# Layer 1 of a two-layer graph network: six products on constants ahead of the transposes of each turn

## The chip, the cores and the metric

The kernel runs on one core of a Trainium2 chip. The metric is the device time of one execution in microseconds; the runs of a kernel are compared by their median. The engines are named as in the profile: PE (TensorE's products), PEld (TensorE's loads of the stationary operand), DVE (VectorE), ACT (ScalarE), POOL (GpSimd) and SP (SyncE, which here issues transfers).

## What is computed

There are 12500 nodes with 48 features and 400000 edges, sorted by their target. Two layers follow each other, each on the normalized, rectified features:

```python
h = jnp.maximum(_layernorm(x, axis=-1), 0.0)
x = x + _L0_gnn_ref(h, edge_index, L0_gnn_W, L0_gnn_b)
h = jnp.maximum(_layernorm(x, axis=-1), 0.0)
x = x + _L1_gnn_ref(h, edge_index, edge_attr_16, ...)
```

Layer 0 is a normalized sum over neighbours with one linear map. Layer 1, in which the change lies, is a small network on every edge and a mean over the edges of a target:

```python
edge = jnp.concatenate([x[source], x[target], edge_feat], axis=-1)
h = jax.nn.relu(edge @ W1 + b1)
h = jax.nn.relu(h @ W2 + b2)
message = h @ W3 + b3
msum = jax.ops.segment_sum(message, target, num_segments=n)
...
update = msum / jnp.maximum(cnt, 1.0)[:, None]
return x + update
```

## The kernel before

The first part of the kernel sorts the edges into runs and computes layer 0; it ends with tables in DRAM: `htab`, the rectified features h of each node, and `btab`, h times the target's part of W1. Then comes the loop of layer 1. It handles the edges in 782 turns c. A turn has four tiles of 128 edges (B = 4; the last turn has one). The steps of a turn are Python functions, and the loop calls them so that four turns are under way at once:

```python
for c in range(NC1 + 3):
    run.append(fetch(c) if c < NC1 else None)
    for step, late in ((summed, 3), (second, 2), (first, 1), (turn, 0)):
        if 0 <= c - late < NC1:
            step(run[c - late])
```

- `fetch(c)` brings in the data. Four indirect transfers that POOL issues (helper `gather`, L208) fetch the source's row of `htab` for each of 128 edges into `et`; these are called the gathers here. ACT copies the edge features into the same tile (L934). DVE compares the targets with the numbers of a window of 40 nodes and writes the result into rows 64 to 103 of the tile `mv` (helper `window_of`, L596), and makes the one-hot tile `oh` for the sum (L941). Once in eight turns SP loads the targets of eight turns, repeated over 40 partitions, into `db` (helper `targets`, L578, 640 KB), with a small load from `wtab_i`, and ACT issues the load of the edge features of eight turns (L923, 256 KB). Every second turn SP loads 40 rows of `btab` into a weight tile (L931).
- `turn` transposes the four tiles of `et` on PE into the PSUM tile `et_ps` (L953), and ACT copies it into rows 0 to 63 of `mv` (L954).
- `first` multiplies `mv` by the weights on PE, 512 edges at once (L959); ACT adds the bias and rectifies (L963).
- `second` multiplies by W2 on PE, four products of 128 columns (L970); DVE takes the maximum with the negative of the bias (L974 and L975).
- `summed` adds the edges into the window's 40 nodes on PE with `oh` as the stationary operand (L990). Every second turn ACT copies the sum out (L999) and SP stores it (L1000).

All of layer 1's operands on PE are f32; layer 0's two products per tile (L793 and L809) are bf16. The profile shows an f32 product as two loads and two passes, a transpose as one.

A scheduler sets the order of each engine's instructions and adds the waits; within an engine the order is fixed. On PE a turn reads: four transposes of turn c, then `summed`, `second` and `first` of the turns behind it, then the transposes of c + 1. On DVE it reads L974, L941, L975, L596. L596 writes a buffer of `mv` that L959 read, so it waits for a product of `first`. The pools have eight buffers of `et`, four of `mv`, and two each of `et_ps` and the other PSUM tiles, which fill all eight banks of PSUM. A gather waits until the transposes of the turn eight before it have read its buffer.

After the loop the two tables of sums are loaded again, multiplied by W3, divided by the counts and added to x.

Of the kernel before, what the change touches and what calls it, by code (L numbers as in the profile page):

```python
# [9 lines left out]
BF = mybir.dt.bfloat16  # L10
# [5 lines left out]
P = 128  # L16
# [4 lines left out]
def kernel(  # L21
# [32 lines left out]
    nc = tc.nc  # L54
# [12 lines left out]
    B = 4  # L67
# [170 lines left out]
    with tc.tile_pool(name="runs", bufs=1) as rp, tc.tile_pool(  # L238
        name="runs_ps", bufs=2, space=bass.MemoryType.PSUM
# [156 lines left out]
    with tc.tile_pool(name="begin", bufs=1) as bp_, tc.tile_pool(  # L396
        name="begin_ps", bufs=1, space=bass.MemoryType.PSUM
# [58 lines left out]
        with tc.tile_pool(name="ln0", bufs=2) as lp, tc.tile_pool(  # L456
            name="ln0_ps", bufs=2, space=bass.MemoryType.PSUM
# [187 lines left out]
    with tc.If(fast > 0) as branch:  # L645
# [6 lines left out]
        with tc.tile_pool(name="tiles", bufs=2) as wp, tc.tile_pool(  # L652
            name="tiles_ps", bufs=2, space=bass.MemoryType.PSUM
# [6 lines left out]
            for h0 in range(0, NS, HG):  # L660
# [31 lines left out]
                for h in range(n):  # L692
# [9 lines left out]
                    for g in range(NC8):  # L702
# [4 lines left out]
                            start=(g == 0),  # L707
                            stop=(g == NC8 - 1),
# [14 lines left out]
            for k in range(2):  # L723
# [5 lines left out]
                    start=True,  # L729
                    stop=True,  # L730
# [13 lines left out]
        with tc.tile_pool(name="e0", bufs=4) as wp, tc.tile_pool(  # L744
            name="n0", bufs=2
# [107 lines left out]
    with branch.Else():  # L853
        with tc.tile_pool(name="deg", bufs=2) as dp, tc.tile_pool(
            name="deg_ps", bufs=1, space=bass.MemoryType.PSUM
# [27 lines left out]
        with tc.tile_pool(name="s0", bufs=2) as wp, tc.tile_pool(  # L883
            name="s0_ps", bufs=1, space=bass.MemoryType.PSUM
# [21 lines left out]
    with tc.If(fast > 0) as branch:  # L906
        with tc.tile_pool(name="e1", bufs=3) as wp, tc.tile_pool(
            name="e1_ps", bufs=2, space=bass.MemoryType.PSUM
# [4 lines left out]
            for k in range(WB):  # L913
                nc.sync.dma_start(wk[k][:F], w1[:F])
                nc.sync.dma_start(wk[k][F:64], w1[2 * F :])
            ea_view = edge_attr[:E4].rearrange("(c p j) f -> p c j f", p=P, j=B)
            def fetch(c):
                n = B if c < NCH else TAIL
                if c % VG == 0:
                    group["db"] = targets(wp, 64, c)  # L920
                    v = min(VG, NCH - c)
                    ea = wp.tile([P, VG, B, EF], FP, name="ea", bufs=2)
                    nc.scalar.dma_start(ea[:, :v], ea_view[:, c : c + v])  # L923
                    group["ea"] = ea
                db, ea = group["db"], group["ea"]
                if c == NCH:
                    nc.scalar.dma_start(ea[:, c % VG, 0, :], edge_attr[E4:])
                if c % Q == 0:
                    group["at"] = window_at(db, 64, c)
                    wc = wk[c // Q % WB]  # L930
                    nc.sync.dma_start(wc[64:], btab[bass.ds(group["at"], W), :])  # L931
                at, wc = group["at"], wk[c // Q % WB]
                et = wp.tile([P, B, 64], FP, name="et", bufs=8)
                nc.scalar.activation(et[:, :n, F:], ea[:, c % VG, :n, :], AF.Copy)  # L934
                for j in range(n):
                    t = c * B + j
                    gather(et[:, j, :F], htab, src_i[:, t : t + 1])
                mv = wp.tile([K1, B * P], FP, name="mv", bufs=4)
                window_of(db, 64, c, mv[64:, : n * P])
                oh = wp.tile([P, B, W], FP, name="oh", bufs=6)  # L940
                nc.vector.tensor_tensor(  # L941
                    oh[:, :n],
                    rel[:, c * B : c * B + n].unsqueeze(2).to_broadcast([P, n, W]),
                    iota_f[:, None, :W].to_broadcast([P, n, W]),
                    OP.is_equal,
                )
                return dict(c=c, n=n, at=at, wc=wc, et=et, mv=mv, oh=oh)

            def turn(k):
                n, et, mv = k["n"], k["et"], k["mv"]  # L950
                et_ps = ps.tile([64, B * P], FP, name="et_ps")
                for j in range(n):
                    nc.tensor.transpose(et_ps[:, j * P : (j + 1) * P], et[:, j, :], ident)  # L953
                nc.scalar.activation(mv[:64, : n * P], et_ps[:, : n * P], AF.Copy)  # L954
# [48 lines left out]
# [5 lines that stand above are left out]
        with tc.tile_pool(name="m1", bufs=2) as npool, tc.tile_pool(  # L1008
            name="m1_ps", bufs=2, space=bass.MemoryType.PSUM
# [39 lines left out]
    with branch.Else():  # L1049
        with tc.tile_pool(name="s1", bufs=2) as wp, tc.tile_pool(  # L1050
            name="s1_ps", bufs=1, space=bass.MemoryType.PSUM
# [3 lines left out]
            with tc.For_i(0, NT, 1) as iv:  # L1055
# [9 lines left out]
                et_ps = ps.tile([IN1, P], FP, name="et_ps")  # L1065
# [72 lines left out]
```

## Time and profile before

| | |
|---|---|
| median of nine runs | 6188.61 us (6176.88 to 6193.04) |
| the profiled execution | 6170.85 us, with a span of 6169.0 us from the first to the last instruction |
| gathers of layer 1, first start to last end | 2054.2 to 6045.8 us, 3125 of them |
| mean of a gather | 972 ns |
| busy in the whole span: PE, PEld | 4410.7 us (71%), 3335.8 us (54%) |
| busy in the whole span: DVE, ACT, POOL | 3164.2 us (51%), 2301.0 us (37%), 3164.1 us (51%) |
| mean clock granted to TensorE | 0.944 of full speed |

A row of a group gives the line, the engine, the operation, the tile it writes and the tiles it reads, the number of instructions, then the busy time and the mean of one in ns, then the idle time of the engine just before them and what ended most of it. A row of the timeline gives the start in us, the duration in us, the engine, the line, the operation, and in brackets the idle time before it and what ended that. Several neighbouring instructions of one group stand in one row (x4).

### The profile page before, as it was taken

How to read it: one execution, taken by the hardware profiler on the slowest of the kernel's cores; microseconds unless marked ns; L12 is line 12 of the kernel's file. 1: busy time of each engine (PE TensorE's matmuls, PEld its weight loads, DVE VectorE, ACT ScalarE, POOL GpSimd, SP SyncE). 2: the span in 40 equal slices, each digit the busy share in tenths (PEclk: the TensorE clock that was granted, in tenths of full speed). 3: DMA queues.
4: the chain of work that ended last, by engine and by line, in shares of the span. 5: the costliest groups of instructions: out<-in, count | busy, mean ns of one | idle time of the engine just before them, and what ended most of it. 6: DMA issues, size and time to landing. Idle time of an engine off the chain costs nothing.

```text
span 6169.0 us, 97254 instructions
## 1 busy us (share of the span) xinstructions
PE 4410.7 (71%) x35368; PEld 3335.8 (54%) x35368; DVE 3164.2 (51%) x4843; ACT 2301.0 (37%) x4904; POOL 3164.1 (51%) x3239
## 2 busy tenths in 40 slices
PE   0001559999999777777777777777777777777776
PEld 0001449999999555555555555555555455554555
DVE  3898489999999433333333333333333333333333
ACT  0001228888888432333323332332333322333331
POOL 0000700000000577777777777777777777777771
PEclk9999869999999899999999999999999999999996
DMA  2002134444444222222222222222222222222224
GB/s 69 2 0 99 31 81 151 147 146 147 147 146 146 65 48 46 48 44 48 48 46 45 47 48 46 48 44 48 46 48 44 48 48 46 46 46 48 47 40 105
DMA packets 397107, 407.58 MB, mean 66 GB/s; under 512 B 227481, under 2 KB 350957, under 8 KB 392110
## 3 DMA queue, kind: packets, MB, share of 16 engines
q1 hardware_dynamic: 155238, 273.99, 15.6%
q0 software_dynamic: 103488, 85.03, 8.0%
q10 hardware_dynamic: 137894, 42.24, 2.9%
q8 instruction: 283, 4.64, 0.3%
q14 instruction: 204, 1.67, 0.1%
HBM read 362.97 MB, written 38.02 MB: 65 GB/s over the span
## 4 chain that ended last, share of the span: by engine, by line
DMA 30%; PE 22%; POOL 16%; DVE 14%; issue 9%; ACT 6%; another core or an unknown queue 2%; POOLq 0%; ACTq 0%; DVEq 0%
DMA et<-htab,src_i 29%; POOL et L208 15%; PE u_ps L990 7%; ACT rows L797 5%; PE sum L809 3%; PE et_ps L953 3%; DVE kb L346 3%; DVE ka L346 3%; PE h_ps L970 3%; DVE ohs L781 2%; PE at_ps L793 2%; DVE oht L777 1%; PE h_ps L959 1%; DVE ohr L695 1%
## 5 line engine op out<-in xcount | busy, mean ns | idle before, releaser
L208 POOL DMA_INDIRECT et<-htab,src_i x3125 | 3038.7, 972 | 2228.5 <-PE tb L636 1275.5
L953 PE MATMUL et_ps<-ident,et 128*64 128x128 f32 x3125 | 690.7, 288 | 942.4 <-DMA et<-htab,src_i 929.8
L953 PEld LDWEIGHTS et_ps<-ident,et 128*64 128x64 f32 x3125 | 347.8, 111 | 1667.0 <-DMA et<-htab,src_i 998.3
L963 ACT ACTIVATE h<-h_ps,b_sb 128x512 f32<-128x512 f32 x782 | 537.2, 687 | 1600.7 <-PE h_ps L959 1599.2
L809 PE MATMUL sum<-rows,ohs 128*128 128x144 bf16 x10976 | 1008.5, 228 | 20.4 <-ACT rows L797 17.4
L797 ACT ACTIVATE rows<-at_ps 128x432 bf16<-128x432 f32 x1830 | 953.9, 531 | 144.7 <-DVE g L756 35.1
L974 DVE MEMSET h<- 128x4 f32 x782 | 48.5, 62 | 1839.5 <-PE u_ps L990 1839.5
L970 PE MATMUL h_ps<-w_sb,h 128*128 128x128 f32 x6250 | 981.3, 304 | 0.5 <-ACT h L963 0.5
L970 PEld LDWEIGHTS h_ps<-w_sb,h 128*128 128x128 f32 x6250 | 827.5, 206 | 169.4 <-ACT et L934 132.1
L990 PE MATMUL u_ps<-h,oh 128*40 128x129 f32 x6250 | 912.9, 292 | 0.0
L809 PEld LDWEIGHTS <-ohs 128*128 128x128 bf16 x10976 | 855.4, 144 | 25.8 <-issue 19.4
L975 DVE TENSOR_TENSOR h<-h_ps,b_neg 128x512 f32<-128x512 f32 x782 | 540.6, 691 | 585.4 <-PE h_ps L970 585.4
L954 ACT ACTIVATE mv<-et_ps 64x512 f32<-64x512 f32 x782 | 459.7, 588 | 984.9 <-PE et_ps L953 984.7
L959 PE MATMUL h_ps<-mv,wk 104*128 104x512 f32 x1564 | 824.6, 609 | 0.0
L781 DVE TENSOR_TENSOR ohs<-lo_b,iota_x 128x4096 bf16<-128x4096 bf16 (+1 forms) x350 | 786.0, 2246 | 51.1 <-PE sum L809 32.8
L990 PEld LDWEIGHTS u_ps<-h,oh 128*40 128x40 f32 x6250 | 678.5, 122 | 123.4 <-issue 34.3
L793 PE MATMUL at_ps<-g,oht 112*128 112x144 bf16 x5488 | 651.3, 226 | 35.9 <-DVE oht L777 35.5
L596 DVE TENSOR_SCALAR mv<-db,wid 40x512 f32<-40x512 int32 x782 | 534.3, 684 | 181.2 <-PE h_ps L959 170.9
L793 PEld LDWEIGHTS <-oht 112*128 112x128 bf16 x5488 | 416.2, 98 | 39.0 <-issue 35.9
L468 PE MATMUL tp<-ident,ht 128*48 128x128 f32 x98 | 25.7, 415 | 415.1 <-ACT ht L383 415.1
L208 POOL DMA_INDIRECT fine<-ltab,where_i x50 | 46.7, 934 | 506.4 <-ACT h_t L470 491.4
L941 DVE TENSOR_TENSOR oh<-rel,iota_f 128x160 f32<-128x160 f32 x782 | 256.1, 328 | 13.3 <-DMA wk<-in_L_gnn_W_dram 2.7
(190 smaller groups left out, 2374.3 us busy)
## 6 DMA issues: line engine op xcount, KB each, us to landing
at<-dltab SPq DMA_DIRECT2D x343, 448.0 KB
db<-in_dst_dram SPq DMA_DIRECT2D x97, 640.0 KB
et<-htab,src_i POOLq DMA_INDIRECT x3125, 2.4
ea<-in_edge_attr_dram ACTq DMA_DIRECT2D x97, 256.0 KB
utab<-zero SPq DMA_DIRECT2D x14, 903.0 KB
utab<-u SPq DMA_DIRECT2D x391, 20.2 KB
wk<-btab SPq DMA_DIRECT2D x391, 20.0 KB
uk<-utab SPq DMA_DIRECT2D x7, 903.0 KB
```

What stands on the lines that cost most here:

```text
L208: nc.gpsimd.indirect_dma_start(out=into, out_offset=None, in_=table, in_offset=bass.IndirectOffsetOnAxis(ap=idx, axis=0),)
L596: nc.vector.tensor_scalar(to.rearrange("p (j i) -> p j i", j=n), db[p0 : p0 + W, a : a + n * P].rearrange("p (i j) -> p j i", j=n), wid[p0 ...
L781: nc.vector.tensor_tensor(ohs[:, :n], lo_b[:, h0 : h0 + n, None, c : c + CG].to_broadcast([P, n, S, CG]), iota_x[:, None].to_broadcast([P, ...
L793: nc.tensor.matmul(ps3[:, i, :], oht[:, k, c % CG, :], g3[:, c, :], start=True, stop=True)
L797: nc.scalar.activation(rows[:, : len(tiles)], ps3[:, : len(tiles)], AF.Copy)
L809: nc.tensor.matmul(sums[k][:, j, :], ohs[:, k, j * P : (j + 1) * P, c % CG], rows[:, i, :], start=(c == 0 and j == 0), stop=(c == ND - 1 a ...
L953: nc.tensor.transpose(et_ps[:, j * P : (j + 1) * P], et[:, j, :], ident)
L959: nc.tensor.matmul(h1_ps[:, : n * P], k["wc"], k["mv"][:, : n * P], start=True, stop=True)
L963: nc.scalar.activation(h1[:, : n * P], h1_ps[:, : n * P], AF.Relu, bias=b1_sb)
L970: nc.tensor.matmul(h2_ps[:, j, :], h1[:, j * P : (j + 1) * P], w2_sb, start=True, stop=True)
L975: nc.vector.tensor_tensor(h2[:, :n, :H], h2_ps[:, :n], b2_neg[:, None, :].to_broadcast([P, n, H]), OP.max,)
L990: nc.tensor.matmul(u_ps, oh[:, j, :], h2[:, j, :], start=(q == 0 and j == 0), stop=(q == Q - 1 and j == n - 1),)
```

## The change

Ahead of the loop, DVE sets a bf16 tile `fill` of 128 x 512 to zero. In each turn, ahead of the four transposes, PE multiplies this tile by its own first 64 columns six times, into the PSUM tile `et_ps` that the transposes of that turn then overwrite. Each product has 128 rows, 64 stationary columns and 512 moving columns; nothing reads their results. In the changed kernel the lines behind the insertions are numbered 3 higher in `fetch` and 5 higher below the loop over the products; L596, in a helper above, keeps its number.

```diff
@@ -913,6 +913,9 @@
             for k in range(WB):
                 nc.sync.dma_start(wk[k][:F], w1[:F])
                 nc.sync.dma_start(wk[k][F:64], w1[2 * F :])
+            fill = wp.tile([P, B * P], BF, name="fill", bufs=1)
+            nc.vector.memset(fill, 0.0)
+            FILL = 6
             ea_view = edge_attr[:E4].rearrange("(c p j) f -> p c j f", p=P, j=B)
@@ -949,6 +952,8 @@
             def turn(k):
                 n, et, mv = k["n"], k["et"], k["mv"]
                 et_ps = ps.tile([64, B * P], FP, name="et_ps")
+                for _ in range(FILL):
+                    nc.tensor.matmul(et_ps, fill[:, :64], fill, start=True, stop=True)
                 for j in range(n):
                     nc.tensor.transpose(et_ps[:, j * P : (j + 1) * P], et[:, j, :], ident)
                 nc.scalar.activation(mv[:64, : n * P], et_ps[:, : n * P], AF.Copy)
```

## The prediction

> **What bounds the kernel now.** I read first the page, for the share of the layer-1 loop; then the table by stretches, for its ends and its clock; then the waits of POOL, to see whether anything holds up the gathers; last the timeline of a few turns, one instruction at a time. The page:
>
> ```profile
> span 6169.0 us, 97254 instructions
> ...
> L208 POOL DMA_INDIRECT et<-htab,src_i x3125 | 3038.7, 972 | 2228.5 <-PE tb L636 1275.5
> L953 PE MATMUL et_ps<-ident,et 128*64 128x128 f32 x3125 | 690.7, 288 | 942.4 <-DMA et<-htab,src_i 929.8
> ...
> L596 DVE TENSOR_SCALAR mv<-db,wid 40x512 f32<-40x512 int32 x782 | 534.3, 684 | 181.2 <-PE h_ps L959 170.9
> ```
>
> The gathers run from 2054 to 6046 us. The stretch's row, with busy time of PE, PEld, DVE, ACT and POOL, then the granted clock:
>
> ```profile
> 2054.00:6046.00 3992.00, 3049.71 (x17140) 2033.36 (x17140) 1377.77 (x3125) 1202.62 (x2731) 3038.67 (x3125) 0.95 0.23 47
> ```
>
> What POOL waited for between 2100 and 6040 us (total, times, longest):
>
> ```profile
> POOL et L208 <- issue: 719.0, 2359, 0.3
> POOL et L208 <- PE u_ps L990: 88.7, 291, 0.3
> POOL et L208 <- DMA et<-htab,src_i: 66.1, 217, 0.3
> ```
>
> Whatever name stands there, the pause between two gathers is 0.30 us. So POOL is never held up: 3125 gathers of 0.972 us and 0.30 us between them are 3975 us, the stage but for its first turns. A turn (four gathers) takes 5.00 us at the shortest, 4 x (0.945 + 0.305), and 5.10 on average. PE waits for the landings (942 us on L953); its work isn't the bound.
>
> But the gathers are not all alike. Timeline of a late turn and the one after it, POOL and L596 alone:
>
> ```profile
> 3933.95 0.95 POOL L208 DMA_INDIRECT et<-htab,src_i  x1 [0.31 <-issue]
> ...
> 3935.05 0.69 DVE L596 TENSOR_SCALAR mv<-db,wid 40x512 f32<-40x512 int32 x1 [0.82 <-PE h_ps L959]
> ...
> 3935.20 1.36 POOL L208 DMA_INDIRECT et<-htab,src_i  x1 [0.30 <-PE et_ps L953]
> ...
> 3938.12 1.13 POOL L208 DMA_INDIRECT et<-htab,src_i  x1 [0.31 <-issue]
> ...
> 3938.45 0.68 DVE L596 TENSOR_SCALAR mv<-db,wid 40x512 f32<-40x512 int32 x1 [0.17 <-PE h_ps L959]
> ```
>
> A gather that should take 0.945 us takes 1.36 and 1.13 where L596 lies badly. Call p the time from the start of the latest gather to the start of L596. Over all 782 turns of the timeline: with p from 0.14 to 0.43 that gather is longer by p - 0.13 (**first place**: 0.33 gives 0.19); with p from 0.68 to 1.15 the next gather is longer by p - 0.68 (**second place**: 1.10 gives 0.42); elsewhere nothing. These sum to 82 us of the 84 by which the gathers exceed 3125 x 0.945. So what can change the time is where L596 falls, and L596 starts 0.2 us after the last pass of `first` (L959): PE sets it.
>
> The Trainium skill's GPSIMD Engine Reference, section Specifications, says that GpSimd's SBUF interfaces are shared with VectorE, with contention from instructions in a 2-port mode or with two SBUF inputs. It would count L941 too; in the trace a gather beside L941 alone is longer by 0.15 us at most, nearly always by nothing. I count L596 alone.
>
> **How PE places L596 today.** In an ordinary turn PE waits for the fourth gather's landing; L596 starts 3.30 us after the last transpose, always at nearly the same p: 464 turns have p between 0.56 and 0.87, and cost 0.033 us each (15 us). After a late landing PE runs without waiting, and L596 comes every 3.40 us (3935.05 to 3938.45). In 140 turns L596 comes over 5.6 us after the one before it, in sum 342 us later than at 5.0; most follow the 640 KB load of db, issued once in 8 turns, 0.71 us after L596. 170 of these 342 us are the pieces from transposes to L596 that took some 4.9 us instead of 3.3, at half the granted clock after PE's wait. The other 318 turns cost 68 us.
>
> **The change, part by part.** The memset is one DVE instruction before the loop, 0.3 us, beside the first gathers' latency. In the order of instructions, six load-and-multiply pairs stand between `first` and the transposes of each of 782 turns; otherwise PE, DVE, ACT and POOL keep their order in the loop, and SP issues the small load of wtab_i a little sooner. The first product of a turn waits for its et_ps buffer, as the transposes did; ACT (L954) read that two turns earlier. The transposes still wait for the landings, now behind the products; behind them are the same `summed`, `second` and `first`, and with these L596.
>
> *Price of a product.* No bf16 product of 512 columns is in the trace. Nearest row: L959, two passes of 512 columns in f32, starts 0.433 us apart, 0.866 a product. In f32, 129 columns cost 0.224 us (L990, two passes 0.112 apart); in bf16, 144 columns cost 0.0645 (L809). Per column that is 1.74 against 0.45 ns, a factor of 3.9. So a product is 0.866/4 = 0.217 us by the nearest row, 0.229 by L809 stretched to 512 columns; six are 1.30 to 1.37. I take 1.30, since L959 has the same width. Could the loads not overlap? In L809 they do (load 0.144 busy, pair 0.0645). If none did, at 0.098 each (L793's), six would be 1.89: the far end.
>
> *What hides it.* PE waits about 1.6 us in an ordinary turn, from the end of `first` to the last landing, less the transposes. 1.30 fits in; 0.3 us is left, and p stays at 0.69. No wait goes away from POOL.
>
> *What it costs after a late landing.* PE's own turn is 3.40 + 1.30 = 4.70. L596 in the second place delays the next gather by p - 0.68, so the next p is p + 4.70 - 5.00 - (p - 0.68) = 0.38: the first place, and that for every such p. From the first place the next p is p + 4.70 - 5.00 - (p - 0.13) = -0.17, i.e. 1.08 after the gather before: the second place. A pair that repeats as long as PE is behind, at 0.25 + 0.40 = 0.65 us per two turns, 0.325 a turn. (With 3.40 the same formula gives 0.33 after the second place: the fence shows 3938.45 - 3938.12.) PE catches up 0.30 by itself and 0.325 because the gathers are slowed, 0.625 a turn, where it now has 1.6 and more. So 52% of all lateness becomes lengthened gathers.
>
> *Sum.* Lateness: 172 us without the half-clock pieces, 342 with all. The wait that precedes a half-clock piece was about 2.8 us and becomes 1.5, less than waits of ordinary turns now, so I leave out five sixths of the 170: 200 us. Catch-up turns: 200/0.625 = 320, cost 104 us; the other 462 at 0.033, 15 us. Together 119 against 82: +37. At the end, six products stand before the last transposes: at most +1.3, I count 1. Sum +38 us on the profiled execution, which took 6170.85 (span 6169.0): 6209. The median of the nine runs is 17.8 us above it; I put the same 38 on 6188.6: **6227 us**. Ends of this case: with 172 us, 89 + 17 - 82 = +24, and +10 if a quarter of that is caught up at rival A's pace; with all 342, 178 + 8 - 82 = +104, +105 with the tail.
>
> The Trainium skill's page TensorE: Matmul & The Clock Gate, section HAM oscillation, says that idle gaps over about 3.4 us throttle the array and that PE should be kept busy. The row agrees in kind: clock 0.95 in this stage. By that rule the change gains whatever half-clock time costs on the path, up to 170 us here; by the row of POOL's waits, that time is not on the path, and it gains 0.
>
> **Rivals.** *A, the pair breaks: faster.* If a turn is over 4.77 (products over 1.37 together, the upper end above), the p after the second place passes 0.45, where L596 no longer delays (0.43 still does, 0.47 doesn't). L596 then drifts over all places, 0.083 us a turn on average at this pace: 172/0.383 = 449 turns, 37 us, and 333 at 0.033, 11: 48 against 82, -34, so 6155. Nearer to 5.00 a turn it stays longer in the free places, down to nothing lost: -80, 6109. For it: the edge is only 0.07 us away. Against: L959 says 1.30. Decides at 4.77.
>
> *B, nothing to be seen.* Lateness is recovered by waits I do not foresee and pairs are rare: +1 from the tail, bounds -11 to +12, 6190. For it: POOL is the bound and PE has the room. Against: the fence shows both places one after the other already.
>
> *C, PE becomes the bound.* At 1.89, a turn takes 5.29: 782 x (5.29 - 5.10) = +149, 6338. It begins over 5.10, i.e. 1.70 for six. Against: the loads overlap in L809.
>
> **How the numbers follow.** Main case 0.64, A 0.18, B 0.12, C 0.06. About 0.2%, 12 us, is what a measurement of this kernel can tell from no change. Slower: main and C, less 0.02 for the main case's low end: 0.68. Within: B, that 0.02 and 0.01 of A: 0.15. Faster: 0.17. The range reaches from 6165, the upper part of A, over B to 6293, the main case's +105; it leaves out the rest of A and C. The main case alone: 6199 to 6294.
>
> **What would show it.** Right: gathers' mean up from 972 to about 983 ns (945 + 119 us/3125), pauses still 0.30; products starting 0.217 us apart; L596 every 4.70 us after a late landing, with p alternating near 0.38 and 1.08; clock near 1.0 in the stage. Wrong: products over 0.228 us, p past 0.45, a gather mean under 972 (A); mean unchanged (B); POOL pausing for PE (C).

## The result, and the profile after

The changed kernel takes 6205.83 us (median of 9 runs, 6200.75 to 6207.13). The kernel before, timed beside it in 29 runs, takes 6183.39. The ratio is 1.0034, with an interval of 1.0026 to 1.0042: some 21 us slower. The forecast was 38 us. The time lies in the range and the direction came as forecast, but the forecast size was nearly twice what came, and the direction came by a path that neither the main case nor a rival had (below). The profiled execution took 6196.64 us (span 6194.9).

The page of the changed kernel (busy time, mean of one, idle time ahead and its releaser):

```profile
span 6194.9 us, 105865 instructions
...
L208 POOL DMA_INDIRECT et<-htab,src_i x3125 | 3064.8, 981 | 2206.3 <-PE tb L636 1253.9
L956 PE MATMUL et_ps<-fill 128*64 128x512 bf16 x4692 | 1164.5, 384 | 4.9 <-DVE fill L917 4.0
...
L596 DVE TENSOR_SCALAR mv<-db,wid 40x512 f32<-40x512 int32 x782 | 569.3, 728 | 164.7 <-PE h_ps L964 155.6
L958 PE MATMUL et_ps<-ident,et 128*64 128x128 f32 x3125 | 517.1, 282 | 119.1 <-DMA et<-htab,src_i 118.8
```

The gathers' mean went from 972 to 981 ns, 26 us over 3125 gathers; the stage from the first gather's start to the last one's end went from 3991.6 to 4017.3 us; what lies behind it stayed at 123.2 us. PE's wait for the landings, 942 us in front of the transposes, is down to 119: the products fill it. L596 itself takes 728 ns in place of 684.

The same stretch of the table by stages (busy time of PE, PEld, DVE, ACT, POOL; granted clock; DMA share; GB/s):

```profile
2054.00:6046.00 3992.00, 3867.96 (x21682) 2296.70 (x21682) 1409.82 (x3110) 1213.53 (x2718) 3045.23 (x3105) 0.99 0.23 47
```

The clock rose from 0.95 to 0.99: the half-clock pieces of the stage fell from 108 (392 us) to 12 (51 us). That bought nothing. The rule that the prediction weighed, the Trainium skill's TensorE: Matmul & The Clock Gate, section HAM oscillation, is borne out in kind, for less idle time went with a higher clock. Its figure is not: of the 108 pieces before, only 4 came within 7 us after a wait of PE of over 3.4 us (the longest wait in those 7 us is 2.3 us in the median, where the prediction has 2.8), and the changed kernel still has such pieces though no wait of PE between 2100 and 6040 us is over 2.34 us. The time went the way of the row of POOL's waits. In the changed kernel's waits of POOL, 2100 to 6040 us, the pause is still 0.3 us, whoever is named:

```profile
POOL et L208 <- issue: 727.8, 2388, 0.3
POOL et L208 <- DMA et<-htab,src_i: 117.0, 384, 0.3
```

So GpSimd still sets the pace and is never held up; only its gathers got longer. The timeline of four turns, lines chosen:

```profile
4000.12 0.94 POOL L208 DMA_INDIRECT et<-htab,src_i  x1 [0.30 <-issue]
4000.20 1.02 PE L964 MATMUL h_ps<-mv,wk 104*128 104x512 f32 x2
4001.16 1.48 PE L956 MATMUL et_ps<-fill 128*64 128x512 bf16 x6
4001.26 0.71 DVE L596 TENSOR_SCALAR mv<-db,wid 40x512 f32<-40x512 int32 x1 [0.17 <-PE h_ps L964]
4001.37 1.43 POOL L208 DMA_INDIRECT et<-htab,src_i  x1 [0.31 <-PE h_ps L964]
4002.57 0.63 PE L958 MATMUL et_ps<-ident,et 128*64 128x128 f32 x4
...
4005.60 0.94 POOL L208 DMA_INDIRECT et<-htab,src_i  x1 [0.30 <-issue]
...
4006.19 0.74 DVE L596 TENSOR_SCALAR mv<-db,wid 40x512 f32<-40x512 int32 x1 [0.17 <-PE h_ps L964]
...
4009.28 0.33 DVE L944 TENSOR_TENSOR oh<-rel,iota_f 128x160 f32<-128x160 f32 x1
4009.34 1.08 POOL L208 DMA_INDIRECT et<-htab,src_i  x1 [0.30 <-issue]
...
4010.73 1.24 POOL L208 DMA_INDIRECT et<-htab,src_i  x1 [0.30 <-issue]
...
4011.12 0.72 DVE L596 TENSOR_SCALAR mv<-db,wid 40x512 f32<-40x512 int32 x1 [0.17 <-PE h_ps L964]
```

L596 comes every 4.93 us, not every 4.70 (4001.26, 4006.19, 4011.12). From `first` to the first product are 0.96 us, from there to the transposes 1.41, together 2.37; two passes of 0.433 and six products of 0.217 would be 2.17. And the phases (p, from the start of the latest gather to that of L596) are not the predicted pair. At p 1.14 (4001.26 less 4000.12) the next gather takes 1.43 us (0.48 longer); one turn on, at 0.59 (4006.19 less 4005.60), L596 touches nothing, but the one-hot L944 lengthens a gather by 0.13; at 0.39 (4011.12 less 4010.73) the gather is longer by 0.29.

### The profile page after: what moved, and what is told of

It is laid out like the page before. It is cut to its first block, busy times and chain, and to the rows that moved or that the text cites. A ratio compares the mean times of both kernels' runs of the same rounds, so it can differ in the third digit from the quotient of the medians.

```text
span 6194.9 us, 105865 instructions
## 1 busy us (share of the span) xinstructions
PE 5256.5 (85%) x40060; PEld 3615.8 (58%) x40060; DVE 3202.3 (52%) x4844; ACT 2319.4 (37%) x4904; POOL 3211.8 (52%) x3239
## 4 chain that ended last, share of the span: by engine, by line
PE 45%; DMA 16%; DVE 14%; POOL 9%; issue 6%; ACT 6%; another core or an unknown queue 2%; POOLq 0%; ACTq 0%; DVEq 0%
DMA et<-htab,src_i 16%; PE et_ps L956 10%; PE h_ps L975 8%; POOL et L208 8%; PE u_ps L995 8%; PE h_ps L964 7%; ACT rows L797 5%; PE et_ps L958 5%; PE sum L809 3%; DVE kb L346 3%; DVE ka L346 3%; DVE ohs L781 2%; PE at_ps L793 2%; DVE oht L777 1%
## 5 line engine op out<-in xcount | busy, mean ns | idle before, releaser
L956 PE MATMUL et_ps<-fill 128*64 128x512 bf16 x4692 | 1164.5, 384 | 4.9 <-DVE fill L917 4.0
L956 PEld LDWEIGHTS <-fill 128*64 128x64 bf16 x4692 | 453.1, 110 | 933.5 <-issue 599.5
L975 PE MATMUL h_ps<-w_sb,h 128*128 128x128 f32 x6250 | 913.3, 290 | 0.5 <-ACT h L968 0.5
L975 PEld LDWEIGHTS h_ps<-w_sb,h 128*128 128x128 f32 x6250 | 763.7, 193 | 152.6 <-ACT et L937 147.6
L995 PE MATMUL u_ps<-h,oh 128*40 128x129 f32 x6250 | 846.8, 277 | 0.0
L995 PEld LDWEIGHTS u_ps<-h,oh 128*40 128x40 f32 x6250 | 640.0, 116 | 147.9 <-issue 132.6
L596 DVE TENSOR_SCALAR mv<-db,wid 40x512 f32<-40x512 int32 x782 | 569.3, 728 | 164.7 <-PE h_ps L964 155.6
L958 PE MATMUL et_ps<-ident,et 128*64 128x128 f32 x3125 | 517.1, 282 | 119.1 <-DMA et<-htab,src_i 118.8
L958 PEld LDWEIGHTS et_ps<-ident,et 128*64 128x64 f32 x3125 | 284.5, 111 | 474.6 <-issue 317.0
```

Source lines behind the costliest of these rows:

```text
L596: nc.vector.tensor_scalar(to.rearrange("p (j i) -> p j i", j=n), db[p0 : p0 + W, a : a + n * P].rearrange("p (i j) -> p j i", j=n), wid[p0 ...
L956: nc.tensor.matmul(et_ps, fill[:, :64], fill, start=True, stop=True)
L975: nc.tensor.matmul(h2_ps[:, j, :], h1[:, j * P : (j + 1) * P], w2_sb, start=True, stop=True)
L995: nc.tensor.matmul(u_ps, oh[:, j, :], h2[:, j, :], start=(q == 0 and j == 0), stop=(q == Q - 1 and j == n - 1),)
```

## The experiments

**The chips.** Three of the runs (i1 to i3) fell on a chip where the kernel before takes 6190 us, the others on chips where it takes 6970 to 7086 us. On those, ScalarE and VectorE often start long after the end of the matmul that they wait for; such starts are called late signals here, though no run shows that the signal itself is what is late. In the first two profiles every evacuation (the instruction that reads a result out of PSUM) that waited for `first` alone starts 37 or 38 ns after the matmul's end, but for three in each that start 97 or 98 ns after it. In f3, with five products:

```profile
3005.02 0.63 PE L958 MATMUL et_ps<-ident,et 128*64 128x128 f32 x4
...
3008.27 0.95 POOL L208 DMA_INDIRECT et<-htab,src_i  x1 [0.30 <-issue]
...
3010.76 0.59 ACT L959 ACTIVATE mv<-et_ps 64x512 f32<-64x512 f32 x1 [3.62 <-remote]
3010.89 0.06 DVE L979 MEMSET h<- 128x4 f32 x1 [3.76 <-remote]
...
3011.47 0.95 POOL L208 DMA_INDIRECT et<-htab,src_i  x1 [2.25 <-ACT mv L959]
```

The transposes end at 3005.65; ACT starts to evacuate them 5.1 us later, idle for the last 3.62 of these, and DVE is let go 0.13 us after it; only then is a buffer free for POOL. In each such profile 600 to 960 of the stage's 2346 evacuations start over 0.3 us late (half of those by over 1.9 to 2.7 us, a tenth by over 4.0 to 5.6, run by run), and POOL stands 780 to 1000 us beyond its 0.30 us pauses. (f1's expectation names a clock of 0.82 in e1 to e4 and TensorE as the pace there. The clock is 0.82 in e1 alone, 0.92 to 0.94 in the other three.) On these chips GpSimd isn't the bound, and a total says little about the theory. What can be read from them is what one instruction costs: the gathers' mean and the distances on PE.

| run | kernel | ratio to before there (interval) | gathers' mean, ns | PE's turn, us |
|---|---|---|---|---|
| e1 | comparison on ScalarE | 1.009 (1.006 to 1.012) | 945 | 3.40 |
| e2 | the same, six products | 1.022 (1.017 to 1.027) | 946 | 4.93 |
| e3 | five products | 1.023 (1.020 to 1.026) | 997 | 4.71 |
| e4 | six, and 160 columns | 1.021 (1.017 to 1.025) | 990 | 5.00 |
| f1 | no comparison | 1.001 (0.998 to 1.004) | 948 | 3.40 |
| f2 | no comparison, six products | 1.015 (1.011 to 1.019) | 946 | 4.93 |
| f3 | five products | 1.009 (1.006 to 1.012) | 1000 | 4.71 |
| f4 | six, and 160 columns | 1.025 (1.021 to 1.028) | 996 | 5.00 |
| g1 | one float32 product | 1.029 (1.019 to 1.038) | 992 | 4.52 |
| h1 | products to a spare tile | 1.022 (1.020 to 1.023) | 995 | 4.93 |
| h2 | the changed kernel | 1.018 (1.016 to 1.020) | 989 | 4.93 |
| i1 | ScalarE paces (6190 us chip) | 6162.3 us, one run | 966 | - |
| i2 | the kernel before (6190 us chip) | 6195.9 us, one run | 980 | 3.40 |
| i3 | products of 128 columns (6190 us chip) | 6226.9 us, one run | 990 | 4.69 |
| j1 | products of 128 columns | 1.020 (1.017 to 1.023) | 1001 | 4.69 |
| j2 | six, and 160 columns | 1.022 (1.019 to 1.025) | 994 | 5.00 |
| j3 | no comparison | 1.001 (0.999 to 1.003) | 945 | 3.40 |
| j4 | no comparison, six products | 1.018 (1.013 to 1.024) | 946 | 4.93 |

The same kernel on two of the slower chips differs by 1.4% (e3 and f3): there the totals cannot be ranked by the length of the turn.

**Is it L596 that lengthens the gathers?** e1 and e2 move the comparison to ScalarE; f1, f2, j3 and j4 leave it out.

```diff
-        nc.vector.tensor_scalar(to..., db..., wid..., None, op0=OP.is_equal)
+        nc.scalar.activation(tv, db..., AF.Square, bias=wid..., scale=-1.0)        # e1, e2
+        nc.scalar.activation(tv, tv, AF.Relu, bias=one_col[...], scale=-1.0)
+        nc.scalar.activation(to, blank[p0 : p0 + W, : n * P], AF.Copy)             # f1, f2, j3, j4
+        nc.scalar.activation(to[:, :B], db[p0 : p0 + W, a : a + B], AF.Copy)
```

e1: 

> The kernel before, with the window's comparison moved from DVE to ACT: Square of (wid - db), then Relu of (1 - that), so that L596 is gone from DVE. Theory 'place' (the gathers set the time, and what lengthens them is where DVE's comparison falls among them): the mean of a gather falls from 972 ns to about 948, since only the one-hot of L941 is left (some 8 us in all), and the time falls by about 75 us, ratio 0.988. Rival 'traffic' (gathers are lengthened by transfers or by anything else that the loop does): the mean stays near 972 and the time within 0.2%.

e2: 

> The changed kernel with the same move of the comparison to ACT. Theory 'place': with nothing on DVE to be placed badly, the six products are free as long as PE's turn (4.93 us in the changed kernel) is under 5.00: the time equals that of the kernel before with the comparison on ACT to within 10 us. Rival 'work' (the products cost time by themselves, by PE's length, the extra instructions or their reads): about 20 us above that kernel, as the changed kernel is above the one before.

f1: 

> The kernel before, with the comparison L596 taken off VectorE: ScalarE copies 512 zeros (and four elements of db) into the window's rows, so layer 1's one-hot of the receiver is left out and the output is not the reference's. Theory (GpSimd's issues are lengthened by where L596 falls on VectorE, 82 us in all): the gathers' mean falls from 972 to 945-948 ns, the pauses between them stay 0.30 us, and the time falls by 75 to 85 us, ratio 0.987. Rival (the late landings and the halved clock set the pace themselves): the gathers get shorter but pauses over 0.30 us appear, and the time falls by less than 30 us. On a chip whose clock lies at 0.82 in this stage, as in the runs e1 to e4, TensorE and not GpSimd would set the pace and neither theory is tried.

f2: 

> The changed kernel with the same edit (the window's rows are zeros from ScalarE; the output is not the reference's). Theory: the products cost time only through where L596 falls beside the gathers; without it the stage is 3125 gathers of 945-950 ns and 0.30 us, TensorE's turn of 4.93 us just fits under four gathers of 5.00 us, and the time equals f1's within 10 us (ratio 0.986 to 0.990). Rival (the turn of 4.93 us itself is what costs): f2 is slower than f1 by about the same 20 to 25 us that the change cost, ratio 0.991 or more.

j3: 

> The kernel before without L596 on VectorE (the window's rows are zeros from ScalarE; the receivers' one-hot of layer 1 is left out). Theory (L596 makes the lengthening): gathers' mean 945-948 ns, 75 to 105 us under the kernel before, ratio 0.983 to 0.988. Rival (late landings and the halved clock set the pace themselves): less than 30 us under, ratio over 0.995.

j4: 

> The changed kernel without L596 on VectorE (the same part left out). Theory (the products cost time only through where L596 falls): the same time as j3 within 10 us, ratio 0.983 to 0.989. Rival (a turn of 4.93 us costs of itself, since it leaves TensorE no slack after a late landing): 15 to 25 us over j3, ratio 0.987 to 0.992.

Their gathers take 945 to 948 ns in the mean, with and without products; the kernels timed beside them that keep L596 on DVE, all with products, take 990 to 1001. (The kernel before was not profiled on these chips.) From the page of j3:

```profile
L208 POOL DMA_INDIRECT et<-htab,src_i x3125 | 2952.8, 945 | 3191.2 <-PE tb L631 1338.9
```

So the mechanism is shown: with L596 off VectorE the gathers take only 5 to 12 us over the floor of 0.945 us in the whole run, against 141 to 175 us where it stays. None of the six gained time. f1 and j3 stayed at the time of before, since POOL there waits for buffers 887 and 900 us beyond its pauses, so that shorter gathers leave the time where it was; in f2 and j4, with TensorE's turn at 4.93 us, it waits 996 and 991 us. That these 90 to 110 us come from the late signals, which the chip of the first profiles does not have, is likely but not shown: it is also what f2's and j4's rival, that the turn costs of itself, would look like. What removing L596 gains in time where GpSimd is the bound was not measured.

**What is the turn made of?** e3, f3, e4, f4 and j2 change the number of products; g1 makes one float32 product of the six; h1 sends them to a tile nobody reads; i3 and j1 do the same with 128 stationary columns.

```diff
-            FILL = 6
+            FILL = 5                                                               # e3, f3
+                nc.tensor.matmul(et_ps[:, :160], fill[:, :64], fill[:, :160], ...)   # e4, f4, j2: a seventh
+            fill = wp.tile([P, B * P], FP, name="fill", bufs=1); FILL = 1           # g1
-                    nc.tensor.matmul(et_ps, fill[:, :64], fill, ...)
+                    nc.tensor.matmul(spare, fill[:, :64], fill, ...)               # h1: spare is [64, 512]
+                    nc.tensor.matmul(spare, fill[:, :P], fill, ...)                # i3, j1: spare is [128, 512]
+                    group["u_ps"] = ps.tile([W, H1], FP, name="u_ps", bufs=1)      # h1, i3, j1: makes room
```

e3: 

> The changed kernel with five products in place of six. PE's turn without waits should be 4.93 - 0.216 = 4.71 us. Theory 'place': this is the pace for which the prediction described the repeating pair (L596 near 0.39 and near 1.09 after a gather's start in turn, 0.3 and 0.45 us lost), as long as PE is behind: 20 to 45 us slower than the kernel before, so no better than six products. Rival 'work': five sixths of the change's cost, about +18 us, and no such pair.

e4: 

> The changed kernel with a seventh, short product of 160 columns in each turn, so that PE's turn without waits is 4.93 + 0.067 = 5.00 us, the length of four undisturbed gathers. Theory 'place': L596 then keeps its place among the gathers from turn to turn; in the first or the second place it would be pushed out by the delay itself, so it comes to rest in a free place, and the gathers lose 5 to 20 us in all instead of 116: about 75 us faster than the kernel before, ratio 0.988, with more work on PE. Rival 'work': slower than with six products, by 0 to 52 us (782 x 0.067).

f3: 

> The changed kernel with five products in place of six. By the trace of after a product costs 0.216 us and the set of them 0.19 to 0.23 us more at its two ends, so the turn is 4.71 us: what the prediction took the six for. The pair of phases that the prediction described (p 0.38 and 1.08 by turns, a gather lengthened by 0.25 and one by 0.40) should then be seen, and the time be 25 to 45 us over before, ratio 1.004 to 1.007. Rival (the lengthening falls with fewer products, since TensorE is behind less of the time): between before and after, ratio 1.000 to 1.003.

f4: 

> The changed kernel with a seventh product over 160 columns: 0.07 us more, so that TensorE's turn is 5.00 us, that of four unlengthened gathers. Theory (what costs is the drift of 0.07 us a turn by which L596 walks through both places in which it lengthens a gather): with no drift L596 rests where it costs nothing, the gathers' mean falls to 945-955 ns, and the time is 50 to 100 us under before, ratio 0.984 to 0.992. Rival (TensorE becomes the bound as soon as its turn reaches 5.00 us, half-clock pieces and late landings come on top): 0 to 40 us over before, ratio 1.000 to 1.006.

j2: 

> The changed kernel with a seventh product over 160 columns: TensorE's turn is 5.00 us, as long as four unlengthened gathers with their pauses. Theory (the change costs what L596's drift of 0.07 us a turn through both places costs): without drift L596 stays where it falls, outside the places for most of the time, the gathers' mean falls to 945-960 ns and the time is 30 to 100 us under the kernel before, ratio 0.984 to 0.995. Rival (TensorE becomes the bound at 5.00 us): 0 to 40 us over before, ratio 1.000 to 1.006.

Turns of PE without waits are 4.71 us with five products, 4.93 with six and 5.00 with the 160 columns more: 0.216 a product (0.217 predicted), on top of 3.40 and something fixed of 0.23. The times, 1 to 2.5% over before on the slower chips, followed no theory; that L596 rests at a turn of 5.00 us was not tried, for L596 was moved about by late signals all the time (gathers' mean 990 to 996 ns).

g1: 

> One product in place of six, and its operands of float32 in place of bfloat16: it takes apart the extra 0.19 to 0.23 us that a turn pays besides the six times 0.216 us. Theory (TensorE pays about 0.09 us when it goes over from float32 operands to bfloat16 ones, and about as much on the way back): with one float32 product the distances from `first` to the product and from the product to the transposes show no such extra; the product takes 0.85 to 0.88 us, as each of the two 128x512 halves in `first` does by the price of float32, and the shortest TensorE turn is 3.40 + 0.86 = 4.26 us (4.2 to 4.3). Rival (the extra belongs to a change of the stationary operand or of the tile written, whatever the type): the same 0.09 us at each end, and a shortest turn of 4.42 to 4.50 us. The time says little here: on a chip with the clock of the runs before and after, 10 to 40 us over before.

```profile
3000.88 1.02 PE L964 MATMUL h_ps<-mv,wk 104*128 104x512 f32 x2
...
3001.83 1.07 PE L956 MATMUL et_ps<-fill 128*64 128x512 f32 x2
...
3002.84 0.63 PE L958 MATMUL et_ps<-ident,et 128*64 128x128 f32 x4
```

The theory fell: with float32 on both sides it is 0.95 us again from `first` to the product (521 ns from its second pass), and 523 ns, not 433, from the product's second pass to the transposes. The two passes themselves start 480 ns apart, not 433. The turn is 4.52, just over the rival's upper edge. So it isn't the type.

h1: 

> The six products go into a PSUM tile of their own that nobody reads (u_ps has one buffer in place of two, to make room), so that no product waits and the first transpose again has both waits, for the gather and for the tile, as in the kernel before. Theory (each of the two new changeovers costs 0.09 us because the first instruction behind it carries a single wait and its weights are not loaded ahead): the distances are 429 ns from the second half of `first` to the first product and 216 ns from the last product to the first transpose (521 and 310 in the changed kernel), and TensorE's turn is 3.40 + 1.30 = 4.70 us, what the prediction took it for (4.61 where the single buffer of u_ps splits a wait off). Rival (the extra belongs to products beside transposes, whatever they wait for): 521 and 310 again and a turn of 4.93 us. In time, on a chip like that of the runs before and after: the repeating pair of phases comes, 25 to 45 us over before, ratio 1.004 to 1.007.

```profile
3000.29 1.02 PE L965 MATMUL h_ps<-mv,wk 104*128 104x512 f32 x2
3001.24 1.00 PEld L957 LDWEIGHTS <-fill 128*64 128x64 bf16 x6 [0.76 <-issue]
3001.24 1.48 PE L957 MATMUL spare<-fill 128*64 128x512 bf16 x6
3002.66 0.63 PE L959 MATMUL et_ps<-ident,et 128*64 128x128 f32 x4
```

This theory fell too: no product waits for anything, and the distances are 521 and 310 ns as before. So it isn't a wait, and not the tile that is written.

h2: 

> The changed kernel itself, on the chip of this call. Theory for a chip on which the kernel before takes about 6183 us: ratio 1.0034 as before. If the kernel before takes about 7000 us here, as in the runs e, f and g, where ScalarE and VectorE see TensorE's signals up to 8 us late: TensorE's turn of 4.93 us has no slack to make such a stop good, so every stop lasts into the stage's end, and the time is 1.5 to 2.5% over before (f4, with a turn of 5.00 us, was 2.5% over, f3, with 4.71 us, 0.9%).

The changed kernel is 1.8% over before here; h1, with the same turn, 2.2%. That is what a turn of 4.93 us costs beside late signals, and it is no second measurement of the change.

i3: 

> As h1, but the products have 128 stationary columns in place of 64 (the spare tile has 128 rows). Theory (a stationary operand of fewer than 128 columns keeps the next group's first weights from being loaded ahead: in the kernel before the changeovers behind the 64 columns of the transposes and the 40 of `summed` cost 0.09 us, those behind the 128 of `second` and `first` nothing): the last product is followed by the first transpose after 216 ns in place of 310, and a turn is about 0.09 us shorter. Rival (it is neither): 310 ns again.

```profile
2131.31 0.94 POOL L208 DMA_INDIRECT et<-htab,src_i  x1 [0.30 <-DMA et<-htab,src_i]
2131.32 1.02 PE L965 MATMUL h_ps<-mv,wk 104*128 104x512 f32 x2
...
2131.75 0.10 PEld L957 LDWEIGHTS <-fill 128*128 128x128 bf16 x1 [0.24 <-issue]
2132.18 1.46 PE L957 MATMUL spare<-fill 128*128 128x512 bf16 x6
2132.38 0.70 DVE L596 TENSOR_SCALAR mv<-db,wid 40x512 f32<-40x512 int32 x1 [0.17 <-PE h_ps L965]
2132.55 1.35 POOL L208 DMA_INDIRECT et<-htab,src_i  x1 [0.30 <-issue]
2133.48 0.60 PE L959 MATMUL et_ps<-ident,et 128*64 128x128 f32 x4
...
2136.71 1.18 POOL L208 DMA_INDIRECT et<-htab,src_i  x1 [0.30 <-issue]
2137.07 0.69 DVE L596 TENSOR_SCALAR mv<-db,wid 40x512 f32<-40x512 int32 x1 [0.17 <-PE h_ps L965]
```

Only the number of stationary columns differs from h1, and both extras are gone: 0.86 us and 1.30 us, in single distances 428 and 216 ns. (The theory foresaw the second only. In half of the turns the trace has one product fewer; the whole way from `first`'s second pass to the transposes is 1.72 us in both halves.) The loads show how: with 64 columns the first load starts with the first product (3001.24), with 128 it starts 0.43 us ahead of it, beside `first` (2131.75 and 2132.18). The turn is 4.69 us: the one that the prediction reckoned with. And with it comes what the prediction said of such a turn: L596 at p 1.07 and 0.37 in alternate turns, with a gather longer by 0.40 and one by 0.24. The time is 6226.9 us against 6189.8 and 6195.9 (i2) of the kernel before on the same chip, +37 and +31 us, and 20 us over the slowest run of the changed kernel, which ran elsewhere. It is one run.

j1: 

> i3 again, timed over several runs. Theory (TensorE's turn of 4.70 us, as the prediction took it, brings the pair of phases p 0.38 and 1.08 and the forecast lengthening): 30 to 45 us over the kernel before, ratio 1.005 to 1.007, clearly more than the changed kernel's 1.0034. Rival (i3's one time was chance; the length of the turn between 4.70 and 4.93 us makes no difference): ratio 1.002 to 1.0045.

j1 was to time i3 over several runs and fell on a slower chip: turn 4.69 us, ratio 1.020, unanswered.

**The kernel before, and the loop without TensorE.**

i2: 

> The kernel before on a chip where it takes about 7000 us. Theory: TensorE's signals reach ScalarE and VectorE up to 8 us after the matmul's end, as in e1 to h2 and unlike in the first profile (37 ns, always), GpSimd waits 700 to 900 us of the stage for buffers, and TensorE, with a turn of 3.40 us, makes a stop good within some turns. Rival (the late signals come with the added matmuls): signals at 37 ns, and the lost 800 us lie elsewhere.

```profile
L208 POOL DMA_INDIRECT et<-htab,src_i x3125 | 3063.4, 980 | 2206.1 <-PE tb L636 1253.8
```

The question did not arise, since this chip has no late signals. (That they do not come with the added matmuls is shown by f1 and j3, which have none and some 960 late starts each.) But the run tells something else: the same kernel has a gathers' mean of 980 ns here and 972 in the first profile, and it takes 6195.92 us in place of 6170.85. From the four profiles with TensorE on chips without late signals, with the sum of what each gather takes beyond 0.945 us:

| run | time, us | sum beyond 0.945 us, us | difference |
|---|---|---|---|
| before | 6170.85 | 89.9 | 6081.0 |
| before (i2) | 6195.92 | 114.5 | 6081.4 |
| after | 6196.64 | 116.3 | 6080.3 |
| 128 columns (i3) | 6226.87 | 144.1 | 6082.8 |

The whole time of the kernel, changed or not, is 6081 us and the lengthening of its gathers, within 2 us, and the two profiles of the kernel before differ by nothing else. They differ as much as before and after do: in i2 the unchanged kernel's gathers lose about what the changed kernel's lose in its one profile (114.5 and 116.3 us).

i1: 

> Layer 1 without TensorE: its four steps are copies on ScalarE in the same order and with the same waits (the landing, the buffers), so nothing of layer 1 is computed; gathers, L596 and the one-hot L944 stay. The chain from the landing to the next L596 is set to 3.40 us, and copies ahead of the landing's read, where the products stand, make the turn about 3.40, 4.70, 4.93 and 5.00 us in the four quarters (195 turns each; the lengths are worked out from two ScalarE rows and may be off by 0.1 to 0.2 us). Theory (GpSimd loses what L596 costs at the phase where it falls, whatever engine sets the phase): lengthening of the gathers over 0.945 us of 0.08-0.13 us a turn in the first quarter (before: 0.105), about 0.15 in the second (the repeating pair, as predicted), 0.11-0.14 in the third (after: 0.127) and under 0.06 in the fourth. Rival (the lengthening goes with TensorE's own traffic): next to none in all four.

```diff
-                    nc.tensor.matmul(...); nc.tensor.transpose(...)      # turn, first, second, summed
+                act(PADS[k["c"] * 4 // NC1])                             # a copy of that many columns on ScalarE
+                act(0, mv[:64, ...], et[:64, :n])                        # waits for the four landings
```

```profile
L208 POOL DMA_INDIRECT et<-htab,src_i x3125 | 3019.3, 966 | 2207.1 <-PE tb L636 1253.8
L596 DVE TENSOR_SCALAR mv<-db,wid 40x512 f32<-40x512 int32 x782 | 544.0, 696 | 2005.1 <-ACT work L954 1997.1
```

The rival falls: without one matmul in the loop the gathers are lengthened by 69.5 us, 0.086 us a turn in the first quarter, within the 0.08 to 0.13 expected. The other quarters came out shorter than set, at 4.20, 4.43 and 4.50 us (the copies were quicker than worked out), and gave 0.085, 0.089 and 0.096 us a turn; the lengths 4.70 to 5.00 were not reached, so they were not tried.

## Why the prediction was right or wrong

**GpSimd bounds the stage, and only the gathers' length moves the time: right.** Pauses are 0.30 us in both kernels, and the table of four profiles accounts for each time in it.

**Products 0.217 us apart and hidden in TensorE's waits: right.** Measured 0.216; the wait of L958 fell from 942 to 119 us. That the half-clock pieces would go, and that this would gain nothing on the path: right (clock 0.95 to 0.99, time up).

**"Six are 1.30 ... I take 1.30": the term that was mis-sized.** Six products of 64 stationary columns cost 1.53 us: 1.30, 0.09 where `first` gives way to them, 0.09 where they give way to the transposes, and about 0.02 more behind each of these (the second product starts 240 ns after the first and not 216, the second transpose 136 after the first and not 109). This is the step that failed: the turn is 4.93 us and not 4.70, and that carries it over the edge of 4.77 us beyond which the pair of phases, from which the 38 us were worked out, does not repeat. The profile of before held the warning: of its four changeovers two, into `summed` and into `second`, cost 0.09 us (202 and 200 ns in place of 109), two nothing. The upper end of the term was put at 1.37, for the rate of the products alone, and the changeovers were put at nothing; with two changeovers like the dear ones it would have been 1.48 at least. g1 and h1 rule out type, wait and target tile; i3 against h1 shows that it goes with 64 columns in place of 128. (j1, on a slower chip as h1 was, has i3's turn too.) With 64 columns the group's first load starts only with its product. Why the products' load does so and that of the kernel before's transposes, 64 columns too and behind the same `first`, does not (428 ns in place of 521) was not found.

**"A pair that repeats as long as PE is behind": right for the turn it was worked out for, and not what the changed kernel does.** i3 has that turn, and there the steps hold one by one: p 1.07 and 0.37 (1.08 and 0.38 predicted), lateness of the turns over 5.6 us 225 us (200), 120 us of lengthening in the turns outside p 0.56 to 0.87, so 53% of the lateness (52%), and a time of 6226.9 us, 31 to 37 us over the kernel before beside it (38). In the changed kernel 4.93 lies past the 4.77 that rival A gave as the point from which the pair breaks. It broke, as A said.

**Rival A's price, 34 to 80 us faster, was wrong.** It let L596 drift evenly over all places. With 0.07 us a turn L596 comes into each place at the end where it costs most (0.45 to 0.48 us at p 1.14, 0.28 to 0.33 at 0.39), is thrown out below by that one gather, and walks on to the next; between the two the one-hot L944 adds 0.13. In the 640 turns outside p 0.56 to 0.87 that is 97 us, 0.152 a turn in place of A's 0.083. PE gains only 0.07 + 0.15 = 0.22 us a turn on the gathers, so 157 us of lateness take some 700 turns to make good; 685 of the 782 turns are in fact 4.9 to 5.3 us long, and there are hardly any free ones left. So the change came out slower although the main case's pair did not repeat and the rival whose condition held forecast faster: that the direction and the range held was luck.

**Why 21 and not 38, then.** In the two profiles of the first chips L596's part of the lengthening went from 82 to 99 us, not to 119. PE is nearly always behind, so that a late landing meets it later (87 late turns and 157 us, against 140 and 342 before, and 138 and 225 in i3), and only 2 us come from the ordinary turns, which cost 18 in i3. Against that stand 17 us of other lengthening, after 8 before; all but 1 us of the 17 lies in 131 gathers beside L944. The prediction counted L596 alone and set that second contender aside. The Trainium skill's GPSIMD Engine Reference, section Specifications, counts operations with two SBUF inputs; L944 is one, and beside it lie 9 of the 26 us by which the two profiles differ. No run takes L944 away. Nor is this split firm: in i2 L596's part is 105 us and the rest 9, without any product.

**The base.** The profiled execution of before (89.9 us of lengthening) was a quick one, 12.5 us below the median of the 29 runs; that of after lies 9.2 below its own. Their difference, 25.8 us, and that of the medians, 22.4, agree only because both were low. By the sum of 6081 us the medians stand for some 102 us of lengthening before and 125 after. That difference is firm, for the slowest of the 29 runs is faster than the fastest of the 9; how it divides between lateness, phases and L944 rests on one profile each.

What stays open: what makes ScalarE and VectorE start late on the slower chips, and whether it is the chip; the time of i3 over several runs; and what a turn of 5.00 us gives on a chip where GpSimd is the bound. No version here that computes all of layer 1 beat the kernel before.

## What to carry to other kernels

Where two engines hinder each other, it is the phase of the hindering instruction that has a price; a free engine's filler work is not free if it sets that phase. Take the length of the turn from the start-to-start distances at its seams, not from the rate inside a group, and if one phase rule has an edge close by (here 4.77 us), work out the time on both sides with the drift that belongs to each. And compare the path's one variable (here the sum of the gathers over their floor) between several runs before trusting a difference of a few tens of microseconds.

## What the runs showed of the hardware that was not expected

Groups of 512-column products with 64 stationary columns, between `first` and the transposes, start 92 ns late and delay the next group by 94 ns (521 and 310 ns in place of 429 and 216), in bfloat16 and alike in float32 (521 and 523 in place of 429 and 433); with 128 columns the distances are 428 and 216, and the group's first load lies 0.43 us ahead of its product in place of starting with it.

On the slower chips ScalarE and VectorE started over 0.3 us after the matmul they waited for in 26 to 41% of the evacuations of the stage, and the latest by 8 to 25 us, run by run. The kernel before took 13 to 14% longer there. It has no profile there; in f1, which is some 980 us over 6081 us and its lengthened gathers, 887 us are POOL's waits beyond its pauses in the stage, 69 lie ahead of the first gather and 22 behind the last. On the chip of i1 to i3 one start in 2346 was late by more than 0.3 us in the kernel before, and two in i3, all early in the stage.
